# Two attention blocks over eight images: the last output projection by seven products, and other places in the order for the first job's steps

## The chip, the cores and the metric

The kernel runs on one core of a Trainium2 chip. The metric is the device time of one execution in microseconds (us); the median of several executions is compared. Everything is fp32. TensorE is called PE here, VectorE DVE, ScalarE ACT, GpSimd POOL and SyncE SP; SP does nothing but issue DMA transfers, and POOL does little besides issuing those that add to their destination.

## The reference, cut to what matters

The input x has 8 images of 512 channels and 1024 positions. Two blocks (layers 0 and 1) of the same form follow each other; only the names of the weights differ.

```python
# x: (8, 512, 1024); 8 groups; 8 heads of 64 channels
xn = (xg - mean) * rsqrt(var + 1e-5)            # over each group of 64 channels
xn = xn * gamma + beta
q, k, v = Wq @ xn + bq, Wk @ xn + bk, Wv @ xn + bv
attn = softmax(q^T k / 8)                        # per head, 1024 x 1024
o = attn @ v
x = x + Wp @ o + bp
```

## The kernel before, in words

**Jobs.** One job is one layer of one image, 16 in all. They run in pairs of images: (image b, layer 0), (b+1, layer 0), (b, layer 1), (b+1, layer 1) for b = 0, 2, 4, 6. Job n is counted from 0. A fast path assumes that softmax needs no subtraction of the maximum; a small check at the end (`judge`, L895 to L904) tells whether the sums stayed in range.

**Stages of a job.** (1) Attention of job n (`Attention`, L744 to L891): 64 steps of 1.71 us on the planner's clock. Each step has 4 score products (L764), one exponential of a 128x1024 tile on ACT (L769, tile `e`), one add of that tile to a running sum on DVE (L779, L781), and 4 value products (L795). Every 8 steps a group ends (`finish`): the sums are reduced (L811), the output goes into the tile that held q (L818), and for each second group the reciprocals go by DMA through DRAM (tiles `r`, `rd`) into a broadcast tile `rb` (two transfers at L857) and L872 multiplies by it. In the very last group all this is done on DVE alone, without DMA. (2) The V projection of job n+1 (`v_phase`, products at L462). (3) The output projection (O) of job n and then the K and Q projections of job n+1 (`deep_phases`, products at L593). Then attention of job n+1 begins.

**Products.** A projection is computed as a 2x2 block product with 7 half-size products in place of 8. `ORDER` (1, 5, 6, 2, 7, 3, 4) is the order in which they run so that few accumulators (banks z, y, u, v) are needed: z takes products 1, 6, 7 and 4, with copies to y after 1 and to u after 6; product 5 has a bank of its own; 2 goes into y, 3 into u. V does so at one level. O, K and Q do it at two: 7 outer products (`OUTER`, 1, 2, 6, 5, 7, 3, 4), each a *chain* of 7 inner ones with a tile `p_c`, where c = 0 to 20 counts the chains of O, K, Q. So for O the tile p_0 holds product 1, p_1 product 2, p_2 product 6, p_3 product 5, p_4 product 7, p_5 product 3 and p_6 product 4. The tiles `p_c` and `e` share one pool of 6 buffers. The second half of a chain's result is written from PSUM by DVE (L607, L609), the first by ACT. Weights and their sums are loaded or made once per layer, kept in DRAM (`keep` for one level, `deep` for two), and fetched into a ring of 7 tiles `w`.

**Adding O's products to x.** x is cut into quarters (half of the channels, half of the positions). `end(c)` says which products go into which quarter: 1 and 2 into (0,0); 6 (with 1 added), 5 and 3 into (0,1); 5 and 7 into (1,1); 7 (with 6 added) and 4 into (1,0). `more(...)` does one such addition: on DVE (L638, a thunk put at the end of the list `outer`), or, with `moved=True`, as an accumulating DMA of 512 KB issued by POOL (L636), which is written down at once. The lists `soon`, `outer` and `extra` give up one thunk at each of two places per chain (after inner products 7 and 3), `soon` before `outer` before `extra`. Every add is thereby written down some chains after its product ends. Two accesses to the same quarter wait for each other in the order in which they are written down.

**What sets the order.** The orders of PE, ACT and DVE instructions are the order in which the Python code issues them. Each engine runs its own list in that order. `later(delay, fn)` puts `fn` on the planner's clock, and `advance(us)` moves that clock on, so that small steps fall between products. `chores` is a table from attention steps to functions, filled by `put(i, fn)` (the next free step if i is taken). SP's and POOL's orders follow from a scheduler.

**Group norm of job 1.** It is done in job 0's attention, as job 1's image is loaded late: sums and squares on ACT (L239, L247), the channels' sums through DRAM to a tile of 8 groups, the group statistics on DVE (L270 to L274) and POOL (L275), out again through DRAM (`dg`, L277) and back as a broadcast (`mr`, L280), scale and offset on DVE (L288 to L290), and four applications on ACT (L295) that write `xn`. The sums `combine` over `xn` and the inner sums (`deep_steps`) follow. In the same attention DVE makes the weight sums of two more factors (L152 to L158, tile `raw`), and each set is stored as a 1.79 MB `keep` (L162).

**The end.** The last job's output projection is `plain_proj`: 64 products of 128x512 with the weights as they are (L733), a DVE addition of bias and x for each of 8 pieces (L737), and a store of each (L741).

Of the kernel before, what the change touches and what calls it, by code (L numbers as in the profile page):

```python
# [9 lines left out]
F32 = mybir.dt.float32  # L10
# [8 lines left out]
P = 128  # L19
B, C, H, W = 8, 512, 32, 32  # L20
# [6 lines left out]
NC = C // P  # L27
NT = S // P
HALF = S // 2
# [7 lines left out]
CH = C // 2  # L37
A11, S3, A12, A22, S1, S2, S4 = range(7)
NW = 7
K, V, Q, O = range(4)  # L40
FACTOR = {1: A11, 2: A12, 3: S4, 4: A22, 5: S1, 6: S2, 7: S3}
ORDER = (1, 5, 6, 2, 7, 3, 4)
OUTER = (1, 2, 6, 5, 7, 3, 4)
QT = HALF // 2
# [26 lines left out]
def fast_path(  # L71
# [10 lines left out]
    nc = tc.nc  # L82
# [8 lines left out]
    ps, turns = {}, [0]  # L91
# [14 lines left out]
    def later(delay, fn):  # L106
        todo.append((clock[0] + delay, fn))

    def advance(us):
        clock[0] += us  # L110
        due = sorted((t for t in todo if t[0] <= clock[0]), key=lambda t: t[0])
        for t in due:
            todo.remove(t)
            t[1]()
# [15 lines left out]
    def bank(half, tag, name):  # L130
        return ps[half][1].tile([P, HALF], F32, tag=tag, name=name)
# [80 lines left out]
    def load_x(b):  # L212
        for cc in range(NC):
            nc.sync.dma_start(xs[b][:, cc, :], x[b, cc * P : (cc + 1) * P, :])
# [316 lines left out]
    def deep_phases(n, extra, outs=None, early=()):  # L531
# [81 lines left out]
        def end(c):  # L613
            which, o = chains[c]
            m = job(which)
            used((m, which, o))

            def p(k):
                return tiles[which, k]

            def add(to_, a, b):
                outer.append(lambda: nc.vector.tensor_add(to_, a, b))  # L622

            if which == O:
                b, layer = jobs[m]
                xt = xs[b]

                def more(oh, sh, part, moved=False):


                    cols = slice(sh * HALF, (sh + 1) * HALF)
                    to_ = xt[:, 2 * oh : 2 * oh + 2, cols]

                    def go():
                        if moved:
                            nc.gpsimd.dma_start(to_, p(part), accum_op=ALU.add)  # L636
                        else:
                            nc.vector.tensor_add(to_, to_, p(part))  # L638
                        parts[oh, sh] -= 1
                        if layer == 1 and parts[oh, sh] == 0:  # L640
                            rows = slice(oh * CH, (oh + 1) * CH)
                            later(8.0 if moved else 2.0, lambda: nc.sync.dma_start(
                                out[b, rows, cols].rearrange("(c p) s -> p c s", p=P), to_
                            ))

                    if moved:
                        go()
                    else:
                        outer.append(go)

                if o == 1:
                    more(0, 0, 1, True)
                elif o == 2:
                    more(0, 0, 2, True)
                elif o == 6:
                    add(p(6), p(6), p(1))
                    more(0, 1, 6)
                elif o == 5:
                    more(0, 1, 5)
                    more(1, 1, 5, m in (0, 2))  # L660
                elif o == 7:
                    add(p(7), p(7), p(6))
                    more(1, 0, 7)
                    more(1, 1, 7)
                elif o == 3:
                    more(0, 1, 3, True)
                elif o == 4:
                    more(1, 0, 4, True)
                return
            d = dst[which]  # L670

            def quarter(oh, sh):
                return d[:, 2 * oh : 2 * oh + 2, sh * HALF : (sh + 1) * HALF]

            if o == 2:
                add(quarter(0, 0), p(1), p(2))
            elif o == 6:
                add(p(6), p(6), p(1))
            elif o == 5:
                add(quarter(0, 1), p(6), p(5))  # L680
            elif o == 7:
                add(p(7), p(7), p(6))
                add(quarter(1, 1), p(7), p(5))
            elif o == 3:
                add(quarter(0, 1), quarter(0, 1), p(3))
            elif o == 4:
                add(quarter(1, 0), p(7), p(4))
# [27 lines left out]
        at = sorted((7 * c + 2 * j, c, j) for c in range(len(chains)) for j in range(7))  # L715
        return [thunk(c, j) for _, c, j in at]

    def plain_weights(n):
        layer = jobs[n][1]
        w = acts.tile([P, NC, C], F32, tag="deep", name="w_last")  # L720
        nc.sync.dma_start(w, wp[layer].rearrange("(cc p) o -> p cc o", p=P))
        return w

    def plain_proj(n, w):

        b, layer = jobs[n]
        xt = xs[b]
        for sh in range(2):
            cols = slice(sh * HALF, (sh + 1) * HALF)
            for oc in range(NC):  # L730
                ps = bank(sh, "zyuv"[oc], f"pp_{n}_{sh}_{oc}")
                for cc in range(NC):
                    nc.tensor.matmul(  # L733
                        ps, w[:, cc, oc * P : (oc + 1) * P], qt[0][:, cc, cols],
                        start=(cc == 0), stop=(cc == NC - 1),
                    )
                nc.vector.scalar_tensor_tensor(  # L737
                    xt[:, oc, cols], ps, out_bias[:, layer, oc : oc + 1], xt[:, oc, cols],
                    ALU.add, ALU.add,
                )  # L740
                nc.sync.dma_start(out[b, oc * P : (oc + 1) * P, cols], xt[:, oc, cols])  # L741
                advance(3.5)

    class Attention:  # L744
        def __init__(self, n):
# [303 lines left out]
    t = sums(0)  # L1049
# [71 lines left out]
    for n in range(-1, len(jobs)):  # L1121
        last = n + 1 == len(jobs)
        outs = None
        if n >= 0:
            chores = {}

            def put(i, fn):
                while i in chores:
                    i += 1
                chores[i] = fn  # L1130

            if last:
                w = plain_weights(n)
            else:
                if n == 0:
                    first_factors(put, [(O, 0), (V, 1)])
                elif n == 1:
                    first_factors(put, [(K, 1), (Q, 1)])
                elif n == 2:
                    first_factors(put, [(O, 1)])  # L1140
                for i, (_, fn) in enumerate(extra):
                    put(2 + i, fn)
                at = (10, 19, 22, 24, 26, 28, 36, 39, 42, 45)
                if n == 0:
                    for i, fn in zip((3, 3, 4, 5, 6, 8, 10, 11, 12, 13, 15), reads):
                        put(i, fn)
                    at = (22, 30, 34, 35, 37, 38, 41, 44, 47, 50)
                for i, fn in zip(at, steps + sums(n + 1)):
                    put(i, fn)
                deep_first = deep_steps(n + 1)  # L1150
                for at, fn in zip((52, 54, 57, 59), deep_first[4:]):
                    put(at, fn)
                put(61, lambda: (extend_plan(n + 1), [fetch() for _ in range(RING)]))
            assert max(chores, default=0) < NT * len(att.groups)
            att.run(chores)
            banks(0, "one")
            banks(1, "one")
            if last:
                advance(100.0)
                advance(100.0)  # L1160
                judge()
                plain_proj(n, w)
                break
            outs = OutputSums(n)
            out_sums(n, outs)
            first = v_phase(n + 1, ORDER)
            for thunk in first[:-1]:
                thunk()
            rest = first[-1:]
            extra = deque()  # L1170
            if jobs[n][1] == 1 and jobs[n][0] + 2 < B:
                extra.append((11, lambda b=jobs[n][0] + 2: (x_tile(b), load_x(b))))
            if n == 1:
                load, bias_steps = make_out_bias(1)
                extra.append((8, load))
                extra.extend((11, fn) for fn in bias_steps)
            if n + 2 < len(jobs):
                reads, steps = norm_steps(n + 2)
                extra.extend((15, fn) for fn in reads)
        both = deep_phases(n + 1, extra, outs, deep_first[:4] if outs else ())  # L1180
        both[0]()
        rest[0]()
        if n < 0:
            later(22.0, lambda: load_x(1))
        for thunk in both[1:-2]:
            thunk()
        banks(0, "two")
        att = Attention(n + 1)
        att.scores(0)
        att.scores(1)  # L1190
        for thunk in both[-2:]:
            thunk()
        banks(1, "two")
# [249 lines left out]
```

## Time and profile before

| | |
|---|---|
| median of 10 runs | 3216.35 us (3214.45 to 3218.15) |
| profiled execution: its time, its span | 3216.58 us, 3214.8 us |
| PE busy | 3194.4 us (99%), clock 1.000 |
| DVE, ACT, POOL busy | 2767.3 (86%), 1902.4 (59%), 99.5 us (3%) |
| DMA | 313.04 MB, mean 97 GB/s |
| first score product of job 0 | 82.86 us |
| first products of the last projection | 3181.31 us |

In the lines of a timeline the columns are the start in us, the busy time in us, the engine, the line of the kernel, the operation with its output and inputs, shapes and count, and in brackets the idle time of that engine before it and what ended it. SPq lines are transfers being issued by SP. A chain's lines are the start, the length and the engine or transfer that the end of the execution depended on in that stretch.

### The profile page before, as it was taken

To read this page: it belongs to the slowest core of one execution; us is meant where nothing else is said; L and a number is where in the kernel's file an instruction comes from. 1 tells how busy PE (TensorE), PEld (TensorE's weight loads), DVE (VectorE), ACT (ScalarE), POOL (GpSimd) and SP (SyncE) were. 2 spreads that over 40 slices of the span, in tenths; PEclk is the share of its full clock that TensorE was granted. 3 is DMA by queue.
4 is the path that set the end of the run, shared out by engine and by line. 5 is a ranking of instruction groups with operands and counts; after the bars stand their busy time and mean duration, and the time that the engine had idled before them with its cause. 6 is when DMAs were issued, how large, how long until landed. Compare 5 with 4: busy or idle time off the path is not lost.

```text
span 3214.8 us, 57636 instructions
## 1 busy us (share of the span) xinstructions
PE 3194.4 (99%) x22870; PEld 1850.1 (58%) x22870; DVE 2767.3 (86%) x3958; ACT 1902.4 (59%) x3038; POOL 99.5 (3%) x93
## 2 busy tenths in 40 slices
PE   9999999999999999999999999999999999999999
PEld 7366384563836638366483754837557374573843
DVE  8897998979889798897988889888897888988876
ACT  4746646466565665656656565565656656566563
POOL 0000000000000000000000000000000000000000
PEclk9999999999999999999999999999999999999999
DMA  8234172350613305034160421505216051150501
GB/s 316 97 104 130 68 210 69 93 170 22 209 28 88 90 27 158 22 104 127 33 210 16 118 67 38 147 16 144 93 45 192 16 142 43 55 130 22 173 22 41
DMA packets 149462, 313.04 MB, mean 97 GB/s; under 512 B 33864, under 2 KB 46784, under 8 KB 148160
## 3 DMA queue, kind: packets, MB, share of 16 engines
q1 hardware_dynamic: 132320, 276.77, 26.8%
q0 software_dynamic: 16864, 32.51, 6.2%
q8 instruction: 181, 2.97, 0.4%
q14 instruction: 97, 0.79, 0.1%
HBM read 224.35 MB, written 51.18 MB: 86 GB/s over the span
## 4 chain that ended last, share of the span: by engine, by line
PE 95%; DVE 3%; DMA 1%; issue 0%; SPq 0%; ACT 0%; DVEq 0%
PE sc L764 28%; PE po L795 27%; PE vd L593 10%; PE zd L593 10%; PE z L462 6%; PE ud L593 4%; PE yd L593 4%; PE v L462 2%; PE y L462 2%; PE u L462 2%; PE pp L733 1%; DMA x<-p 0%; DMA w<-wqkv_dram 0%; DVE w L154 0%; DVE p L609 0%; DMA raw_v<-wqkv_dram 0%
## 5 line engine op out<-in xcount | busy, mean ns | idle before, releaser
L769 ACT ACTIVATE e<-sc 128x1024 f32<-128x1024 f32 x1024 | 1045.9, 1023 | 582.4 <-PE sc L764 487.4
L764 PE MATMUL sc<-q,k 64*64 64x512 f32 x8192 | 1061.7, 590 | 0.0
L795 PE MATMUL po<-e,v 64*64 64x512 f32 x8192 | 1057.2, 589 | 0.0
L781 DVE TENSOR_TENSOR acc<-acc,e 128x1024 f32<-128x1024 f32 x768 | 936.3, 1219 | 57.7 <-ACT e L769 8.8
L795 PEld LDWEIGHTS po<-e,v 64*64 64x64 f32 x8192 | 313.0, 133 | 566.0 <-issue 557.5
L764 PEld LDWEIGHTS sc<-q,k 64*64 64x64 f32 x8192 | 309.7, 133 | 559.1 <-issue 545.4
L593 PE MATMUL vd<-deep,w 128*128 128x256 f32 x900 | 252.6, 380 | 1.4 <-DVE p L609 1.3
L593 PE MATMUL zd<-deep,w 128*128 128x256 f32 x892 | 248.4, 380 | 5.0 <-DVE p L607 2.2
L779 DVE TENSOR_TENSOR acc<-e,e 128x1024 f32<-128x1024 f32 x128 | 156.4, 1222 | 111.3 <-ACT e L769 111.3
L593 PEld LDWEIGHTS zd<-deep,w 128*128 128x128 f32 x892 | 168.9, 190 | 30.4 <-DVE p L607 3.5
L593 PEld LDWEIGHTS vd<-deep,w 128*128 128x128 f32 x900 | 170.6, 190 | 26.4 <-DVE p L609 2.5
L811 DVE TRANSPOSE_TENSOR_REDUCE r<-acc 128x32 f32<-128x1024 f32 x128 | 158.5, 1238 | 0.5
L636 POOL DMA_DIRECT2D x<-p x62 | 74.6, 1211 | 1972.2 <-ACT p L603 1408.1
L593 PE MATMUL vd<-os,w 128*128 128x256 f32 x420 | 118.1, 380 | 1.6 <-DVE p L609 1.5
L622 DVE TENSOR_TENSOR p<-p,p 128x1024 f32<-128x1024 f32 x94 | 114.2, 1215 | 0.0
L462 PE MATMUL z<-w,t 128*128 128x256 f32 x480 | 110.9, 379 | 0.0
L462 PE MATMUL z<-w,xn 128*128 128x256 f32 x480 | 110.1, 382 | 0.0
L413 ACT COPY ud<-vd 128x256 f32<-128x256 f32 x173 | 61.8, 357 | 77.2 <-PE vd L593 69.8
L611 ACT COPY s<-zd 128x256 f32<-128x256 f32 x173 | 64.5, 373 | 71.8 <-PE zd L593 71.7
L475 ACT COPY v<-z 128x512 f32<-128x512 f32 x32 | 18.7, 585 | 148.5 <-PE z L462 148.5
L462 PEld LDWEIGHTS z<-w,xn 128*128 128x128 f32 x480 | 90.0, 190 | 23.8 <-issue 12.2
L413 ACT COPY ud<-zd 128x256 f32<-128x256 f32 x156 | 55.7, 357 | 76.6 <-PE zd L593 75.1
(213 smaller groups left out, 4058.0 us busy)
## 6 DMA issues: line engine op xcount, KB each, us to landing
w<-deep SPq DMA_DIRECT2D x287, 448.0 KB, 3.9
w<-keep SPq DMA_DIRECT2D x129, 256.0 KB, 2.7
x<-p POOLq DMA_DIRECT2D x62, 512.0 KB, 6.6
rb<-rd SPq DMA_DIRECT2D x96, 256.0 KB, 4.1
deep<-w SPq DMA_DIRECT2D x42, 448.0 KB, 3.7
x<-x_dram SPq DMA_DIRECT2D x28, 512.0 KB, 4.5
out_dram<-x SPq DMA_DIRECT2D x28, 512.0 KB, 6.2
keep<-raw SPq DMA_DIRECT2D x5, 1792.0 KB, 7.7
```

The costliest lines, as they stand in the source:

```text
L413: nc.scalar.copy(u, z)
L462: nc.tensor.matmul(ps[:, ti * CH : (ti + 1) * CH], r[:, cc, t0 : t0 + P], w[:, cc, :], start=(start and ti == 0 and cc == 0), stop=(cc == ...
L593: nc.tensor.matmul(ps, lhs[:, FACTOR[i], :], moving[i], start=start, stop=True, skip_group_check=True,)
L611: return chain(product, lambda ps: nc.scalar.copy(s5, ps), put, z, y, u, w)
L622: outer.append(lambda: nc.vector.tensor_add(to_, a, b))
L636: nc.gpsimd.dma_start(to_, p(part), accum_op=ALU.add)
L764: nc.tensor.matmul(sc[h * HD : (h + 1) * HD, j, :], k[r, hp, k0 : k0 + HD], q[r, hp, sh * HALF : (sh + 1) * HALF], start=True, stop=True,)
L769: nc.scalar.activation(e, sc, AF.Exp, scale=SCALE)
L779: nc.vector.tensor_add(acc[g], self.es[i - 1], e)
L781: nc.vector.tensor_add(acc[g], acc[g], e)
L795: nc.tensor.matmul(po[g][j * HD : (j + 1) * HD, h, :], v[r, kc, d0 : d0 + HD], e[r, j, :], start=(kc == 0), stop=(kc == NT - 1),)
L811: nc.vector.tensor_reduce(self.r[:, 0, m, :], self.acc.pop(g).rearrange("p j (b e) -> p (j b) e", e=RP), AX.X, ALU.add, apply_transpose=True,)
```

## The change

It has five parts.

1. The last job's output projection is done by seven products of half size, by halves of the positions (`last_weights`, `last_right`, `last_sums`, `last_proj`). The weights are the kept factors of layer 1, of one level. For each half, 7 products of 8 matmuls of 128x256; ORDER and the banks as elsewhere. The four sums of the first half's positions are chores at steps 44, 47, 50 and 53 of the last attention; those of the second half and `judge` are put on the planner's clock during the projection.
2. The second image's load is put at 32 rather than 22 us on the planner's clock of the first K and Q phase.
3. In job 0's attention the group statistics, the factors, the four applications and the four sums stand at steps 20, 30, 31, 32, 34, 35, 36, 38, 40, 43 (before 22, 30, 34, 35, 37, 38, 41, 44, 47, 50), and the inner sums at 45, 47, 51, 53 (before 52, 54, 57, 59).
4. For m = 0 and 2 (`fresh`), products 1 and 2 are added to quarter (0,0) by DVE through `outer` rather than by a DMA; product 7 is added to (1,1) by a DMA that is itself put into `outer`. For the other jobs nothing changes.
5. The steps that make layer 1's output bias move from the phase after job 1's attention to the one after job 0's.

```diff
--- before.py
+++ after.py
@@ -648,20 +648,24 @@
                     else:
                         outer.append(go)
 
+                fresh = m in (0, 2)
                 if o == 1:
-                    more(0, 0, 1, True)
+                    more(0, 0, 1, not fresh)
                 elif o == 2:
-                    more(0, 0, 2, True)
+                    more(0, 0, 2, not fresh)
                 elif o == 6:
                     add(p(6), p(6), p(1))
                     more(0, 1, 6)
                 elif o == 5:
                     more(0, 1, 5)
-                    more(1, 1, 5, m in (0, 2))
+                    more(1, 1, 5, fresh)
                 elif o == 7:
                     add(p(7), p(7), p(6))
                     more(1, 0, 7)
-                    more(1, 1, 7)
+                    if fresh:
+                        outer.append(lambda: more(1, 1, 7, True))
+                    else:
+                        more(1, 1, 7)
                 elif o == 3:
                     more(0, 1, 3, True)
                 elif o == 4:
@@ -715,31 +719,84 @@
         at = sorted((7 * c + 2 * j, c, j) for c in range(len(chains)) for j in range(7))
         return [thunk(c, j) for _, c, j in at]
 
-    def plain_weights(n):
-        layer = jobs[n][1]
-        w = acts.tile([P, NC, C], F32, tag="deep", name="w_last")
-        nc.sync.dma_start(w, wp[layer].rearrange("(cc p) o -> p cc o", p=P))
+    def last_weights(n):
+        w = acts.tile([P, NW, 2, CH], F32, tag="deep", name="w_last")
+        nc.sync.dma_start(w, factors[O, jobs[n][1]])
         return w
 
-    def plain_proj(n, w):
+    def last_right(sh, o):
+
+        at = slice(sh * QT, (sh + 1) * QT)
+        if o in (4, 5, 6):
+            return tx[0][:, {5: 0, 6: 1, 4: 2}[o], :, at]
+        rows = 0 if o in (1, 7) else 2
+        cols = 2 * sh + (0 if o in (1, 2) else 1)
+        return qt[0][:, rows : rows + 2, cols * QT : (cols + 1) * QT]
+
+    def last_sums(sh):
+
+
+        def start():
+            if sh == 0:
+                tx[0] = acts.tile([P, 3, 2, HALF], F32, tag="t", name="t_last")
+            nc.vector.tensor_sub(last_right(sh, 5), last_right(sh, 7), last_right(sh, 1))
+
+        def second():
+            nc.vector.tensor_sub(last_right(sh, 6), last_right(sh, 3), last_right(sh, 5))
+
+        def third():
+            nc.vector.tensor_sub(last_right(sh, 7), last_right(sh, 3), last_right(sh, 7))
+
+        def fourth():
+            nc.vector.tensor_sub(last_right(sh, 4), last_right(sh, 2), last_right(sh, 6))
+
+        return start, second, third, fourth
+
+    def last_proj(n, w, sh):
 
         b, layer = jobs[n]
         xt = xs[b]
-        for sh in range(2):
-            cols = slice(sh * HALF, (sh + 1) * HALF)
-            for oc in range(NC):
-                ps = bank(sh, "zyuv"[oc], f"pp_{n}_{sh}_{oc}")
-                for cc in range(NC):
+        z, y, u, w5 = (bank(sh, t, f"{t}_last_{sh}") for t in "zyuv")
+
+        def product(o, ps, start):
+            r = last_right(sh, o)
+            for oc in range(2):
+                for cc in range(2):
                     nc.tensor.matmul(
-                        ps, w[:, cc, oc * P : (oc + 1) * P], qt[0][:, cc, cols],
-                        start=(cc == 0), stop=(cc == NC - 1),
+                        ps[:, oc * QT : (oc + 1) * QT],
+                        w[:, FACTOR[o], cc, oc * P : (oc + 1) * P], r[:, cc, :],
+                        start=(start and oc == 0 and cc == 0), stop=(cc == 1),
+                        skip_group_check=True,
                     )
+
+        def quarter(oh, ph):
+            p0 = sh * HALF + ph * QT
+            return xt[:, 2 * oh : 2 * oh + 2, p0 : p0 + QT]
+
+        def chunks(ps):
+            return ps.rearrange("p (a e) -> p a e", a=2)
+
+        def put5(ps):
+            for oh in range(2):
+                nc.vector.tensor_add(quarter(oh, 1), quarter(oh, 1), chunks(ps))
+
+        def put(oh, ph, ps):
+            to_ = quarter(oh, ph)
+            for a in range(2):
+                oc = 2 * oh + a
                 nc.vector.scalar_tensor_tensor(
-                    xt[:, oc, cols], ps, out_bias[:, layer, oc : oc + 1], xt[:, oc, cols],
+                    to_[:, a], chunks(ps)[:, a], out_bias[:, layer, oc : oc + 1], to_[:, a],
                     ALU.add, ALU.add,
                 )
-                nc.sync.dma_start(out[b, oc * P : (oc + 1) * P, cols], xt[:, oc, cols])
-                advance(3.5)
+                nc.sync.dma_start(
+                    out[b, oc * P : (oc + 1) * P, sh * HALF + ph * QT : sh * HALF + (ph + 1) * QT],
+                    to_[:, a],
+                )
+
+        step = chain(product, put5, put, z, y, u, w5)
+        for o in ORDER:
+            step(o)
+            advance(1.72)
 
     class Attention:
         def __init__(self, n):
@@ -1130,7 +1187,9 @@
                 chores[i] = fn
 
             if last:
-                w = plain_weights(n)
+                w = last_weights(n)
+                for i, fn in enumerate(last_sums(0)):
+                    put(44 + 3 * i, fn)
             else:
                 if n == 0:
                     first_factors(put, [(O, 0), (V, 1)])
@@ -1144,11 +1203,11 @@
                 if n == 0:
                     for i, fn in zip((3, 3, 4, 5, 6, 8, 10, 11, 12, 13, 15), reads):
                         put(i, fn)
-                    at = (22, 30, 34, 35, 37, 38, 41, 44, 47, 50)
+                    at = (20, 30, 31, 32, 34, 35, 36, 38, 40, 43)
                 for i, fn in zip(at, steps + sums(n + 1)):
                     put(i, fn)
                 deep_first = deep_steps(n + 1)
-                for at, fn in zip((52, 54, 57, 59), deep_first[4:]):
+                for at, fn in zip((45, 47, 51, 53) if n == 0 else (52, 54, 57, 59), deep_first[4:]):
                     put(at, fn)
                 put(61, lambda: (extend_plan(n + 1), [fetch() for _ in range(RING)]))
             assert max(chores, default=0) < NT * len(att.groups)
@@ -1156,10 +1215,11 @@
             banks(0, "one")
             banks(1, "one")
             if last:
-                advance(100.0)
-                advance(100.0)
-                judge()
-                plain_proj(n, w)
+                for i, fn in enumerate(last_sums(1)):
+                    later(4.1 + 1.5 * i, fn)
+                later(9.9, judge)
+                for sh in range(2):
+                    last_proj(n, w, sh)
                 break
             outs = OutputSums(n)
             out_sums(n, outs)
@@ -1170,7 +1230,7 @@
             extra = deque()
             if jobs[n][1] == 1 and jobs[n][0] + 2 < B:
                 extra.append((11, lambda b=jobs[n][0] + 2: (x_tile(b), load_x(b))))
-            if n == 1:
+            if n == 0:
                 load, bias_steps = make_out_bias(1)
                 extra.append((8, load))
                 extra.extend((11, fn) for fn in bias_steps)
@@ -1181,7 +1241,7 @@
         both[0]()
         rest[0]()
         if n < 0:
-            later(22.0, lambda: load_x(1))
+            later(32.0, lambda: load_x(1))
         for thunk in both[1:-2]:
             thunk()
         banks(0, "two")
```

## The prediction

> **What bounds the kernel now.** I read the page's busy shares and chain first. Below, m is the job whose projection is added to x, and L numbers are those of the kernel before unless marked.
>
> ```profile
> PE 3194.4 (99%) x22870; PEld 1850.1 (58%) x22870; DVE 2767.3 (86%) x3958; ACT 1902.4 (59%) x3038; POOL 99.5 (3%) x93
> PE 95%; DVE 3%; DMA 1%; issue 0%; SPq 0%; ACT 0%; DVEq 0%
> ```
>
> PE is the limit; 214.8 − 194.4 = 20.4 us of idle is all that ordering can return, and what lies ahead of the first product is part of it. Where the idle lies is told by stage windows between the first score products of successive jobs (columns: stretch, length, then PE, PEld, DVE, ACT, POOL busy, clock, DMA share, GB/s):
>
> ```profile
> 82.93:288.18 205.25, 200.24 (x1434) 115.17 (x1436) 179.16 (x273) 126.87 (x208) 8.27 (x6) 1.00 0.38 115
> 288.18:491.20 203.02, 200.31 (x1435) 115.18 (x1437) 188.69 (x310) 119.14 (x192) 6.22 (x5) 1.00 0.42 129
> 491.20:691.60 200.40, 199.12 (x1434) 115.55 (x1438) 178.29 (x269) 119.22 (x192) 7.43 (x6) 1.00 0.40 124
> 691.60:889.81 198.21, 198.21 (x1434) 115.94 (x1437) 170.62 (x237) 119.25 (x192) 6.22 (x5) 1.00 0.34 99
> ```
>
> From the fourth on PE is never idle: nothing can be won there. The first three are 7.0, 4.8 and 2.2 us over 198.21; with the ends these are what the change touches. PE's timeline names the stalls in brackets, and the last projection:
>
> ```profile
> 200.74 1.99 PE L462 MATMUL v<-w,t 128*128 128x256 f32 x8 [1.09 <-DVE q L818]
> 245.10 0.70 PE L593 MATMUL zd<-deep,w 128*128 128x256 f32 x2 [1.05 <-ACT yd L409]
> 250.36 0.70 PE L593 MATMUL zd<-deep,w 128*128 128x256 f32 x2 [1.54 <-DVE p L607]
> 3181.31 27.73 PE L733 MATMUL pp<-q,w_last 128*128 128x512 f32 x64
> ```
>
> DVE's timeline tells why the 250.36 stall exists, and shows the other places the change touches:
>
> ```profile
> 73.85 0.29 DVE L152 TENSOR_TENSOR w<-w 128x128 f32<-128x128 f32 x1 [1.58 <-DMA w<-wqkv_dram]
> 122.85 0.59 DVE L842 TENSOR_REDUCE lt<-r 32x64 f32<-32x256 f32 x1 [1.94 <-DMA r<-r]
> 132.99 1.19 DVE L872 TENSOR_TENSOR q<-q,rb 128x1024 f32<-128x1024 f32 x1
> 248.75 1.23 DVE L638 TENSOR_TENSOR x<-x,p 128x1024 f32<-128x1024 f32 x1 [2.42 <-DMA x<-p]
> 249.89 0.42 DVE L607 TENSOR_TENSOR p<-zd,s 128x256 f32<-128x256 f32 x1
> ```
>
> An add to x stood 2.42 us for an accumulating DMA into the same quarter, the bank read (L607) stood behind it, and PE behind that. In the chain it is `DMA x<-p` at 236.95, 11.78 us long. SP's own timeline:
>
> ```profile
> 127.48 1.29 SPq L857 DMA_DIRECT2D rb<-rd  x2
> 128.81 0.59 SPq L162 DMA_DIRECT2D keep<-raw  x1
> 131.76 0.28 SPq L277 DMA_DIRECT2D dg<-ga  x1
> 136.41 1.11 SPq L280 DMA_DIRECT2D mr<-dg  x2
> ```
>
> dg is a few bytes, issued behind the 1.79 MB keep, and mr, which waits for it, goes out 4.6 us later. The same dg in job 1's attention, with no keep ahead, takes 1.2 us (311.82 to 312.99).
>
> **The Trainium skill.** "TensorE: Matmul & The Clock Gate" (Architectural detail) says ACT and DVE are strict FIFO: the trace agrees (L607 behind L638, above). "DMA: Bandwidth & Descriptors" (Queues, rings and completion order) says descriptors of one ring are consumed in order, and each DMA engine takes turns between rows at packet level. The 4.6 against 1.2 us agrees, and so do the accumulates of POOL: 7.8 to 11.8 us at m=0 where the 16 DMA engines are busy over 90% (224 to 256 us), 5.6 to 6.6 typically in later jobs. Its "Rules for kernel authors" says an access to bytes that an accumulating DMA touches must wait for its semaphore; so the adds on DVE must wait, and the trace shows one that does. Its SWDGE fit, 2.0 us + bytes/436e3, would give 3.2 us for 512 KB; the trace never shows under 5.4, and I use the trace.
>
> **The change, part by part.**
>
> *Last projection.* Removed: 64 records, 27.73 us. Added: 112 records of 128x256. An x16 row of such records advances PE 3.45 us (L462 rows at 202.57 and 206.02), so 112 take 24.2. DVE's chain before them (r, q, rb, q) ends 7.2 us after the start, at 3188.4; then two 0.60 adds for product 5, sums and puts (0.60, 2×0.40, 0.60, 2×0.40) release bank z at about +11.2, while PE wants it for product 4 at +10.35: 0.9 stall. The last two puts are 2×0.44 against one of 0.75: +0.13. Net −27.73 + 24.2 + 0.9 + 0.13 = −2.5; I take **−2.3** (−3 to −1.5). The eight sums on DVE cost nothing on the path: four lie in job 15's attention, where DVE waits 1.5 to 2.2 us per group for exponentials, four are in the chain just counted. Weights of 1.8 rather than 1.0 MB load a whole attention ahead. What follows the last put (issue 0.33, landing 2.4, end 2.4 us) stays.
>
> *x(1) loaded 10 us later.* A weight load issued at 64.97 landed at 73.8 behind four x loads of SP (62.12 to 64.35); DVE waited 1.58 and PE then 1.27 at 75.33 (its restart costs 0.1 more). The new SP order has the weight ahead of x: **−1.4**. x then lands near 78; its first reader (ACT L239) starts at 91.3, so that cover is 13 us.
>
> *Job 0's attention steps.* DVE has no idle from 122.85 to 236.95, so an order of the same DVE instructions alone gains only what fills the 1.94 at 122.85 (the group statistics, 0.8). But two queues change. (1) SP now issues dg and mr, then keep, then the two rb; before, rb went ahead of keep. keep moved data until 135.3 in before; issued at about 127.4 it ends near 134, and rb behind it lands near 136.9 (135 to 138.5). L872 (after: L929) would be ready at 132.2: waits 4.7, less the 0.8 gained, **+3.9** for all of DVE behind it. (2) On ACT the first normalise (L295) moves from behind exponential 35 to behind exponential 32. It waits for `off` (L290), 143.2 in before, now 147.1; exponential 32 ends at 139.5. Exponential 33, and with it DVE's next add and PE's next products, stands behind. Together about +6.2 (4.4 to 7.9), less any slack: none on DVE, which sets PE's stalls at 200.74, 228.11 and 232.04, so it is passed on: **+6.2**. Lower bound −0.8, were neither wait there.
>
> *x += p at m = 0 and 2.* Products 1 and 2 leave POOL (two accumulates of 512 KB less) for two DVE adds of 1.13 each; one DVE add of product 7 leaves for POOL. DVE +1.1 per job, covered only as far as it has idle. More important is the order. The accumulates of products 3 and 4 (tiles p_5, p_6) are recorded when their product ends, but the longer list of DVE adds is still being popped one at a time. So in the instruction order after, DVE has x += p_3 waiting for the p_5 accumulate into the same quarter, and two adds later x += p_4 waiting for that of p_6. p_5 in turn is issued only when the previous add to its quarter is done, just ahead; p_6 when its own second half is written, which stands behind x += p_3. Both landings therefore lie in series on DVE, L5 and L6. Behind the two adds stand the bank reads L607 of p_7 and L609 of p_8, and PE's zd and vd products behind those. DVE does 2.1 us of other work within the landings and would without the waits be 1.2 ahead of PE: loss L5 + L6 − 3.3. m=0: p_5 goes out at about 243.4, in the saturated stretch: L5 = 8.0 (7.8 to 9.2 seen there); by p_6 the stalled SP stream drains, L6 = 6.2 (as later jobs). 10.9, less the stalls removed (1.05, 1.54, 0.2 restarts) = **+8.1**. m=2: p_5 at 649.65, where the nearest accumulate (648.99) took 10.0; with one fewer beside it 9.3; 9.3 + 6.2 − 3.3 = **+12.2** (7.8 to 16); nothing was waiting there before.
>
> *Output bias of layer 1 one job earlier.* Four 0.68 us multiply-sums (L970, 464 to 477) leave job 1's K/Q phase, whose PE waits of 0.63 and 0.38 (at 469.94 and 483.60, restarts counted) go: **−1.1**, part of it doubtful. They land in 262 to 285, where DVE idles 0.5 to 1.1 per chain. One statistics step moves into job 1's attention: **+0.3**.
>
> Sum: −2.3 − 1.4 + 6.2 + 8.1 + 12.2 − 1.1 + 0.3 = **+22.0**. The profiled run of before was 3216.58 (span 3214.8 and 1.8 around it), 0.23 above the median 3216.35; I add the difference to the median: **3238**. All low ends together give about +10, all high ones +31.
>
> **Rivals.**
> (a) *The adds do not wait; the change does what it says.* The accumulates would have to land within about 0.5 us of their issue, or DVE have that much other work. Then −2.3 − 1.4 − 2.8 (stalls at m=0) − 2.4 (start of job 0) − 1.1 = −10: **3206**, faster. Against: the smallest landing seen is 5.4; turning point: L5 + L6 under about 3.3 and no rb wait.
> (b) *rb is not held by keep* (its packets take turns): job 0 gives +1.5 from the moved normalise alone: **3233**. For: rb reads DRAM in another pattern. Against: dg's 4.6.
> (c) *Only one add waits in earnest, or both landings are 5.4.* With 5.4 twice, m=0 and 2 lose 3.4 and 4.7 less (3230); with L6 hidden, 6.2 less each (3226): **3228**.
> (d) *Landings of 11 and 8 in both,* since the SP stream does not drain: 15.7 in place of 10.9 and 12.2: **3246**.
>
> **How the numbers follow.** Main case 0.50, (b) 0.15, (c) 0.17, (d) 0.10, (a) 0.04, mixtures near zero 0.04. 0.2% is 6.4 us, about what a measurement of this kernel can tell. Faster 0.04 (a), same 0.04, slower 0.92. Range 3223 to 3248: the main case's own bounds, with (b), (c), (d).
>
> **What would show it.** In after's trace: DVE adds L638 at m=0 and 2 with `<-DMA x<-p` of about 7 and 5 us each, PE stalls of 7 and more behind them; a wait of 4 to 5 us for `rb` at L929 near 132, and ACT L295 ahead of exponential 33 waiting; the stage windows at about 219.5, 202, 212.5 and then 198.21 unchanged; the last products 25 us. If the second add waits under 1 us, the series argument is wrong; if stage one is under 207, both queues were misread.

## The result, and the profile after

The kernel after takes 3235.58 us (median of 8 runs, 3234.38 to 3237.43); the kernel before, run beside it, 3215.95 (28 runs, 3214.36 to 3220.52). The ratio is 1.0061, 95% interval 1.0053 to 1.0070: slower by 19.6 us. The profiled execution took 3237.88 us with a span of 3236.0. It is 2.3 us above its median, and most of that lies behind the last instruction on DVE: 3236.0 − 3229.33 = 6.67 us here, against 3214.8 − 3209.84 = 4.96 before and 4.4 to 4.9 in the traces of the eleven other kernels below, which have the same new end. One execution of all those reported, of the kernel with keep later, took 5229 us for a reason that is not known; the intervals leave it out.

The page's first row and its row of clocks (tenths of full speed in 40 slices) look almost as before, as an average over 3236 us must:

```profile
PE 3195.9 (99%) x22918; PEld 1861.8 (58%) x22918; DVE 2777.2 (86%) x3980; ACT 1904.9 (59%) x3042; POOL 95.6 (3%) x91
PEclk9999999999999999999999999999999999999999
```

The stage windows between first score products tell where the time is (stretch, length, busy time of PE, PEld, DVE, ACT, POOL, clock, DMA share, GB/s):

```profile
81.60:301.60 220.00, 203.57 (x1432) 115.92 (x1431) 182.47 (x283) 127.14 (x208) 5.53 (x5) 0.97 0.37 111
301.60:502.75 201.15, 199.28 (x1431) 115.48 (x1431) 187.09 (x302) 119.15 (x192) 6.22 (x5) 1.00 0.41 124
502.75:713.31 210.56, 201.76 (x1432) 117.15 (x1431) 178.84 (x269) 119.25 (x192) 6.26 (x5) 0.98 0.38 116
713.31:911.52 198.21, 198.21 (x1432) 115.94 (x1431) 170.62 (x237) 119.26 (x192) 6.22 (x5) 1.00 0.34 99
```

Against before: start −1.26 (82.86 to 81.60; the program ran 0.27 late already at 46 us, so the later load is worth 1.53), first stage +14.75, second −1.87, third +10.16, the fourth equal to the hundredth, and from the first product of the last projection to the end of its last put 26.24 for 28.53, −2.29. The sum is +19.5. PE's timeline names the stalls (stretches in which PE stands still), in brackets:

```profile
147.34 1.98 PE L821 MATMUL sc<-q,k 64*64 64x512 f32 x8 [5.92 <-ACT e L826]
...
260.65 1.22 PE L593 MATMUL zd<-deep,w 128*128 128x256 f32 x2 [8.06 <-DVE p L607]
...
266.87 0.70 PE L593 MATMUL vd<-deep,w 128*128 128x256 f32 x2 [1.19 <-DVE p L609]
...
672.36 1.22 PE L593 MATMUL zd<-deep,w 128*128 128x256 f32 x2 [7.00 <-DVE p L607]
...
3214.33 1.99 PE L765 MATMUL z_last<-t_last,w_last 128*128 128x256 f32 x8 [0.61 <-DVE x L787]
```

And DVE's timeline tells what PE stood for. At m = 0:

```profile
248.35 0.47 DVE L609 SCALAR_TENSOR_TENSOR p<-zd,out_bias,s 128x256 f32<-128x256 f32 x1
257.51 1.22 DVE L638 TENSOR_TENSOR x<-x,p 128x1024 f32<-128x1024 f32 x1 [8.68 <-DMA x<-p]
258.65 0.48 DVE L609 SCALAR_TENSOR_TENSOR p<-ud,out_bias,s 128x256 f32<-128x256 f32 x1
259.05 1.21 DVE L622 TENSOR_TENSOR p<-p,p 128x1024 f32<-128x1024 f32 x1
260.18 0.42 DVE L607 TENSOR_TENSOR p<-zd,s 128x256 f32<-128x256 f32 x1
264.86 1.23 DVE L638 TENSOR_TENSOR x<-x,p 128x1024 f32<-128x1024 f32 x1 [4.27 <-DMA x<-p]
```

Two adds, two waits, one behind the other, and in between the bank reads that PE wants. At m = 2 the same pair waits 7.62 and 4.27 us. In job 0's attention there are two more, on DVE for rb and on ACT for the offset, and behind the second DVE waits for the exponential (147.32):

```profile
134.81 1.23 DVE L929 TENSOR_TENSOR q<-q,rb 128x1024 f32<-128x1024 f32 x1 [3.72 <-DMA rb<-rd]
...
144.94 0.16 DVE L290 TENSOR_TENSOR off<-vec_sb,off 128x4 f32<-128x4 f32 x1
...
147.32 1.23 DVE L836 TENSOR_TENSOR acc<-e,e 128x1024 f32<-128x1024 f32 x1 [2.22 <-ACT e L826]
```

```profile
137.27 1.02 ACT L826 ACTIVATE e<-sc 128x1024 f32<-128x1024 f32 x1 [0.71 <-DVE acc L838]
145.14 1.24 ACT L295 ACTIVATE xn<-x,off,mul 128x1024 f32<-128x1024 f32 x1 [6.84 <-DVE off L290]
146.28 1.00 ACT L826 ACTIVATE e<-sc 128x1024 f32<-128x1024 f32 x1
```

The second fence is ACT's timeline: exponential 32, then the normalise, then exponential 33, which PE's 5.92 us stand for. SP's timeline has the order as forecast, mr and keep ahead of rb:

```profile
123.59 1.75 SPq L280 DMA_DIRECT2D mr<-dg  x2
125.44 0.54 SPq L162 DMA_DIRECT2D keep<-raw  x1
126.08 2.05 SPq L914 DMA_DIRECT2D rb<-rd  x2
```

### The profile page after: what moved, and what is told of

It reads as the page before. It is cut to its first block, busy times and chain, and to the rows that moved or that the text cites. A ratio compares the mean times of both kernels' runs of the same rounds, so it can differ in the third digit from the quotient of the medians.

```text
span 3236.0 us, 57775 instructions
## 1 busy us (share of the span) xinstructions
PE 3195.9 (99%) x22918; PEld 1861.8 (58%) x22918; DVE 2777.2 (86%) x3980; ACT 1904.9 (59%) x3042; POOL 95.6 (3%) x91
## 4 chain that ended last, share of the span: by engine, by line
PE 78%; DVE 1%; issue 0%; DMA 0%; ACT 0%; DVEq 0%; POOLq 0%
PE sc L821 22%; PE po L852 22%; PE vd L593 9%; PE zd L593 9%; PE z L462 5%; PE ud L593 4%; PE yd L593 4%; PE y L462 1%; PE u L462 1%; PE v L462 1%; PE z_last L765 0%; DVE acc L838 0%; DMA x<-p 0%; DVE q L929 0%; DVE x L787 0%
## 5 line engine op out<-in xcount | busy, mean ns | idle before, releaser
L638 DVE TENSOR_TENSOR x<-x,p 128x1024 f32<-128x1024 f32 x75 | 91.1, 1215 | 24.8 <-DMA x<-p 24.8
L462 PEld LDWEIGHTS z<-w,xn 128*128 128x128 f32 x480 | 90.0, 190 | 23.8 <-issue 12.2
```

Of the source, the lines that this page charges most:

```text
L462: nc.tensor.matmul(ps[:, ti * CH : (ti + 1) * CH], r[:, cc, t0 : t0 + P], w[:, cc, :], start=(start and ti == 0 and cc == 0), stop=(cc == ...
```

## The experiments

In all of them the times of before are of runs on the same chips (medians 3216.12 to 3216.26). "Stage" is a window as above.

**Part 4 undone.**

```diff
-                fresh = m in (0, 2)
+                fresh = False
-                    more(1, 1, 5, fresh)
+                    more(1, 1, 5, m in (0, 2))
```

> After, with part 4 (x += p at m = 0 and 2) undone. Theory (two adds on DVE wait in series for accumulating DMAs, PE stands behind): job 0's stage loses 8.4 us of its 220.0, the third stage returns to about 200.4 (from 210.6); about 3217, PE's stalls of 8.06 and 7.00 gone and the old ones of 1.05 and 1.5 back. Rival (the loss at m = 0 is carried over from the attention steps, as DVE comes late): m = 0 stays long, only the third stage recovers: about 3225.

3217.39 us, ratio 1.0002 (0.9994 to 1.0011). First stage 211.51, third 200.11: 8.49 and 10.45 us less. The stalls of 8.06 and 7.00 are gone, the old ones at m = 0 are back (1.94 and 1.05, where before has 1.05 and 1.54). The loss at m = 0 is its own and not carried over.

**Part 3 undone.**

```diff
-                    at = (20, 30, 31, 32, 34, 35, 36, 38, 40, 43)
+                    at = (22, 30, 34, 35, 37, 38, 41, 44, 47, 50)
-                for at, fn in zip((45, 47, 51, 53) if n == 0 else (52, 54, 57, 59), deep_first[4:]):
+                for at, fn in zip((52, 54, 57, 59), deep_first[4:]):
```

> After, with part 3 (the steps of job 0's attention) undone. Theory (rb behind keep in SP's queue, then a normalise ahead of an exponential): job 0's attention recovers about 6.35 us, PE's stall of 5.92 at 147 gone, the adds at m = 0 and 2 still wait as long: about 3229. Rival (DVE is the limit in job 0 and what one place saves the next one takes): under 2 us gained, about 3234.

3230.49 us, ratio 1.0044 (1.0027 to 1.0061). The stall at 147 is gone, the first stage is 213.62 (6.38 less), and the pair of waits at m = 0 is 8.40 and 4.28 as in after. The rival's gain of under 2 us is out.

**Parts 3 and 4 undone** (both edits).

> After, with parts 3 and 4 undone: the last projection by seven products, the later load of x(1) and the earlier bias remain. Theory: these give -2.3, -1.3 and about -1.5, so 3210 to 3212, faster than before by 4 to 6 us. Rival (the later load or the bias cost something that the two large losses hid): 3214 to 3217.

3211.74 us, ratio 0.9987 (0.9980 to 0.9993): 4.4 us faster than before. Stages 206.15, 201.15, 200.13. Parts 1, 2 and 5 together are a gain, and no loss of theirs was hidden behind the two large ones. Part 5 has a run of its own below; parts 1 and 2 were not run apart, and their shares are read from the traces.

**The same work, the DMAs written down in turn.** The transfers of products 3 and 4 also go through `outer`.

```diff
                 elif o == 3:
-                    more(0, 1, 3, True)
+                    if fresh:
+                        outer.append(lambda: more(0, 1, 3, True))
+                    else:
+                        more(0, 1, 3, True)
                 elif o == 4:
-                    more(1, 0, 4, True)
+                    if fresh:
+                        outer.append(lambda: more(1, 0, 4, True))
+                    else:
+                        more(1, 0, 4, True)
```

> After, with the accumulating DMAs of products 3 and 4 also put through the list outer at m = 0 and 2, so that they are written down behind the adds on DVE. Same amount of work on every engine. Theory (the order makes the waits, not the work): no wait of DVE for x<-p over 1 us, the third stage about 200.4, job 0's stage about 209 to 211 (6.35 for the attention steps left): 3214 to 3219. Rival (the extra DVE adds or the shared DMA engines make the loss): above 3228.

3217.56 us, ratio 1.0005 (0.9996 to 1.0014); stages 211.72 and 201.06, where after has 220.00 and 210.56. Every engine has the same instructions. The order alone is worth 18 us. Its DVE timeline, with after's two waiting adds now among the rest:

```profile
249.02 1.22 DVE L638 TENSOR_TENSOR x<-x,p 128x1024 f32<-128x1024 f32 x1
250.15 0.48 DVE L609 SCALAR_TENSOR_TENSOR p<-ud,out_bias,s 128x256 f32<-128x256 f32 x1
250.55 1.22 DVE L622 TENSOR_TENSOR p<-p,p 128x1024 f32<-128x1024 f32 x1
251.68 0.41 DVE L607 TENSOR_TENSOR p<-zd,s 128x256 f32<-128x256 f32 x1
252.01 1.21 DVE L638 TENSOR_TENSOR x<-x,p 128x1024 f32<-128x1024 f32 x1
...
264.70 0.42 DVE L607 TENSOR_TENSOR p<-zd,s 128x256 f32<-128x256 f32 x1 [2.02 <-DMA x<-p]
```

No add waits. What is left are two late buffers: twice a `p` tile is written again 1.8 to 2.4 us late, by DVE (at 264.70 and 269.33) and by ACT (at 264.69 and 269.32), because the DMA that reads it has not landed. This costs PE 0.87 and 1.45 us. So even in this order part 4 gains nothing over part 4 undone (3217.56 against 3217.39): it trades one late transfer for another.

**Only the second add in turn**, with part 3 undone (compare with 3230.49): the edit above for product 4 alone.

> Part 3 undone (3230.5 with only that); the accumulating DMA of product 4 alone goes through outer at m = 0 and 2, that of product 3 still ahead of the add on DVE. Theory (two landings in series): the first wait of 7.6 to 8.7 stays, the second of 4.3 us goes. As PE's stall after the second one was only 1.2 to 1.4, because most of it fell while PE worked again, each job gains 1.0 to 1.5: about 3228. Rival (the waits are one: the second only takes what the first leaves): the first grows and nothing is gained, 3230.

3228.71 us, ratio 1.0038 (1.0023 to 1.0052). That is 1.8 us below 3230.49, but the ranges overlap (3227.6 to 3230.36 in 5 runs, 3229.03 to 3231.72 in 4). The second wait is gone, but at m = 0 the first was 9.93 us here (its DMA landed after 9.7 us, in the other run after 8.2):

```profile
252.90 1.23 DVE L638 TENSOR_TENSOR x<-x,p 128x1024 f32<-128x1024 f32 x1 [9.93 <-DMA x<-p]
255.90 1.22 DVE L638 TENSOR_TENSOR x<-x,p 128x1024 f32<-128x1024 f32 x1
```

PE's stall is 9.31 where the two were 7.78 and 1.38. At m = 2 the first landing hardly differs (8.6 us, in the other run 8.5), and there the first wait stays at 8.81 for 8.64: it does not take over what the second leaves, as the rival had it. PE's stall is 8.19 for 8.02 and 1.25, yet the stage is only 0.64 us shorter (210.97 for 211.61), since PE is at half speed just there (see the part on why the prediction was right). The first wait is what costs; the second adds little to the time.

**Keep later than rb.** With part 4 undone (3217.39) the fourth sum of the first stored factor and its store come five steps later.

```diff
-                put(at, lambda i=i, part=part: factor(box[0][:, i], part))
-            put(at + 1, lambda i=i, which=which, layer=layer: store_factors(
+                put(at + (5 if at == 21 and which_layers[0] == (O, 0) else 0), lambda i=i, part=part: factor(box[0][:, i], part))
+            put(at + (6 if at == 21 and which == O and layer == 0 else 1), lambda i=i, which=which, layer=layer: store_factors(
```

> Part 4 undone (as the run with only that), and job 0's last sum for the first stored factor, with its keep store, five attention steps later, so that SP issues both rb ahead of keep. Theory (keep ahead of rb in one queue makes the wait of 3.7 us at L929): that wait is under 0.5 us; the normalise L295 still stands ahead of exponential 33, but its offset is ready near 141.2, so ACT waits about 3 us instead of 6.8 and PE about 2 instead of 6: job 0's stage about 207, 3212 to 3214. Rival (rb is slow by itself): the wait stays over 3 us, 3217.

3213.91 us, ratio 0.9994 (0.9985 to 1.0003); first stage 208.35, 3.2 less. The wait for rb is 0.66, ACT waits 4.16 us in place of 6.84 and PE 3.16.

**Normalises later.** Part 4 undone, keep as in after.

```diff
-                    at = (20, 30, 31, 32, 34, 35, 36, 38, 40, 43)
+                    at = (20, 30, 34, 35, 36, 37, 38, 39, 40, 43)
```

> Part 4 undone, and the four normalises at steps 34 to 37 rather than 31 to 36 with gaps (sums and inner sums as in the change); keep stays ahead of rb. Theory (two waits in series): the wait for rb stays 3.7 us, the ACT wait of 6.8 goes to under 3.5 (the offset is ready at 145, exponential 35 now ahead of it), PE's stall of 6 becomes 1 to 3: job 0's stage about 207 to 209, 3213 to 3216. Rival (DVE's 3.7 us alone make the whole loss, as DVE has no idle): no gain, 3217.

3215.39 us, ratio 0.9998 (0.9990 to 1.0007); first stage 208.64. The wait for rb stays (4.21), ACT waits 2.19, PE 1.19 there and 2.46 at the end of the attention.

**Both edits.**

> Part 4 undone, with both edits: keep after rb, and the normalises later. Theory: neither wait left; job 0's stage equals that of old steps (206.15) or 0.8 less, as the group statistics fill an idle stretch of DVE: 3210.5 to 3212. Rival (the earlier sums themselves cost): above 3214.

3211.63 us, ratio 0.9987 (0.9980 to 0.9994). First stage 206.40, no stall of PE in the attention's middle. Old steps give 206.15, in a stage that had no half clock of PE, as this one has (last section). The medians, 3211.63 and 3211.74 with 20 runs each, can't be told apart: the earlier sums cost nothing and bring nothing that these runs show.

**Keep from POOL.** Part 4 undone; this was to test the prediction's reason for rb's delay, that SP's queue holds it.

```diff
-        nc.sync.dma_start(keep, w)
+        (nc.gpsimd if (which, layer) == (O, 0) else nc.sync).dma_start(keep, w)
```

> Part 4 undone, the steps of part 3 kept, but the 1.79 MB keep store of job 0's attention is issued by POOL, so that it isn't in SP's queue. The same bytes move at the same time. Theory (order within SP's queue): the wait of DVE for rb at L929 falls from 3.7 us to under 1.5, PE's stall from 6 to about 3. Rival (the DMA engines' time is what lacks): the wait stays over 3 us.

3218.29 us (one run). The wait did not fall. POOL's and DVE's timelines:

```profile
125.44 0.76 POOL L162 DMA_DIRECT2D keep<-raw  x1 [4.38 <-DVE raw L158]
```

```profile
135.16 1.23 DVE L929 TENSOR_TENSOR q<-q,rb 128x1024 f32<-128x1024 f32 x1 [4.11 <-DMA rb<-rd]
```

rb, now with no large transfer ahead of it on SP, took 8.2 us from issue to landing, against 8.0 in after; DVE's wait was 3.80 with part 4 alone undone. The theory as predicted fails here: it isn't the place in SP's queue. rb is late beside the 1.79 MB of keep whichever of the two queues carries them. That the later keep takes the wait to 0.66, and the other queue doesn't, leaves the time of the DMA engines themselves, or of the memory behind them; that is found by elimination, and no run here tells the two apart.

**The bias back.** Parts 3, 4 and 5 undone.

```diff
-            if n == 0:
+            if n == 1:
                 load, bias_steps = make_out_bias(1)
```

> Parts 3, 4 and 5 undone: only the last projection and the later load of x(1). Theory (the bias moved is worth about 1 us): the second stage back at 203.0 from 201.15, the first at 205.25 from 206.15, the start and the end as after: about 3212.7, that is 1 us slower than with the bias moved. Rival (the bias steps' loads are what made the first stage 0.9 longer, and the second gains nothing): 3211 or less.

3212.72 us, ratio 0.9989 (0.9980 to 0.9998). Stages 205.09, 203.04, 200.12 against 206.15, 201.15, 200.13 with the bias moved: 1.9 won in the second, 1.1 given back in the first, 0.8 net; the medians differ by 1.0.

**Product 7 by DMA at m = 0 alone**, on the run with both edits.

```diff
-                    if fresh:
+                    if m == 0:
                         outer.append(lambda: more(1, 1, 7, True))
```

> The run with keep later and the normalises later (3211.6), and at m = 0 product 7 added to (1,1) by a DMA in the order of outer, products 1 and 2 as before the change. One add on DVE fewer (1.13 us), one DMA more. Theory (at m = 0 the adds wait for DMAs, so a DVE add fewer helps only where no buffer comes late): between 3210 (the stall for the add gone) and 3214 (a late buffer in its place). Rival (more accumulates slow one another): over 3215.

3211.37 us, ratio 0.9985 (0.9978 to 0.9992); first stage 205.72, for 206.40. It can't be told from 3211.63. It, the run with both edits, and parts 3 and 4 undone are three forms of the fastest kernel here, 4.4 to 4.9 us below before.

## Why the prediction was right

The sign and the size were right (+22.0 forecast, +19.6 measured), and so was the mechanism of the large losses: adds on DVE that wait for transfers written down ahead of them, and PE behind DVE. The order in which DVE, ACT and SP would run their work came out as forecast. The terms compare as follows.

| term | predicted | measured | from |
|---|---|---|---|
| last projection | −2.3 | −2.29 | 28.53 to 26.24 in the profiles |
| x(1) later | −1.4 | −1.5 | from the product at 46.08 (after: 46.35) to the first score product, 36.78 to 35.25; the stall at 75.33 is gone |
| job 0's steps | +6.2 | +6.4 or +5.4 | 220.0 − 213.62 with part 4, 211.51 − 206.15 without |
| m = 0 | +8.1 | +8.5 | 220.00 − 211.51 |
| m = 2 | +12.2 | +10.45 | 210.56 − 200.11 |
| bias | −0.8 | −0.8 | both stages, run with the bias back |

Some of this closeness is luck, as errors inside the terms cancel.

*Three of the four landings were taken too long, and too much work was taken to lie within them.* L5 and L6 are the landings of the transfers of `p_5` and `p_6`. L5 was 8.5 us at m = 0 for the 8.0 taken, but 7.5 at m = 2 for 9.3, and L6 was 5.1 us in both for 6.2, shorter than any landing in before's trace (5.3 there, where the prediction has 5.4). The 10.0 us of the one at 648.99 in before was not a guide; there the next accumulate went out 3.1 us behind it, in after 9.6 us behind, but no run tests whether that is the reason. On the other side the prediction took 2.1 us of DVE's other work to lie within the landings. It was 0.7 us: the landings add up to 13.6 and 12.6 us, DVE's waits to 12.95 and 11.89. With the measured landings and the 2.1 us left in, the formula gives 7.5 for m = 0 and 9.3 for m = 2, both about 1 us short. DVE's waits less the 1.2 us by which it was taken to be ahead give 11.75 and 10.7, and at m = 0 the old stalls go off that (1.94 and 1.05 in the run without part 4, restarts 0.2): 8.6 and 10.7, for 8.5 and 10.45 measured.

*PE's half clock was not foreseen, but is not a term on top.* Windows over the records behind the stalls at 147.34 and 260.65, with the clock in the third column from the right:

```profile
147.30:149.10 1.80, 1.76 (x9) 0.55 (x13) 1.78 (x2) 1.38 (x2) 0.00 (x0) 0.50 0.00 0
149.10:150.80 1.70, 1.70 (x12) 0.49 (x8) 1.70 (x4) 1.35 (x2) 0.00 (x0) 0.50 0.00 0
...
262.00:264.20 2.20, 2.20 (x6) 1.69 (x6) 0.00 (x0) 1.11 (x3) 0.10 (x1) 0.50 1.11 185
264.20:266.00 1.80, 1.48 (x7) 0.95 (x5) 1.14 (x1) 0.37 (x1) 0.00 (x0) 1.00 1.07 146
```

PE ran at half speed for 3.5 to 5 us. From 260.65 four pairs of products took 3.57 us (to 264.22) where a restart (the first pair behind a stall) and three more pairs take 0.53 + 3 × 0.43 = 1.83 at full speed: 1.7 us more. At 672.36 six pairs took 5.07 for 2.68, 2.4 us more. The Trainium skill has this ("TensorE: Matmul & The Clock Gate", Part 1: The HAM clock gate: half rate after an idle window of about 3.4 us, full rate after as much busy time; here shorter stalls were enough at times, see the last section). The prediction counted stalls as if PE came back at full speed. The page's row of clocks, in tenths, does not show it. PE's own account of m = 2 needs it: 7.00 + 0.55 of stall, 2.4 of slow clock and two restarts of 0.1 are 10.2 of the 10.45. Yet at 266.87 and 678.58 PE stood once more for DVE, and between the two stalls DVE waited for the second landing alone (4.27 us), not for PE. By these traces a PE at full speed would only have stood longer there, and the loss would be the same; no run tests this apart. Where the second wait is missing, as in the run with only the second add in turn, the slow products take its place: at m = 2 six pairs took 5.08 us there, and most of what the second stall had cost was not won.

*The reason for rb's wait was wrong, its size nearly right.* Predicted 4.7, measured 3.72. "rb goes behind keep in SP's queue" is refuted by the run with keep on POOL; what the runs leave is that both move at once. The small transfer dg in before, which led to that reading, fits either account. The other half, a normalise ahead of an exponential on an engine that runs its list in order, is shown twice: later normalises take PE's stall from 6 to 1.2 us, and a keep that is later takes it to 3.16, since the offset is then ready sooner. The two waits are in one chain, so each edit alone saves about 3 us and both together 5.1. DVE's waits again account for the term: 3.72, the 2.22 at 147.32 (2.3 forecast) and one of 1.01 for a later rb at 194.89 that was not forecast, less 0.7 of the old wait at 122.85 that is filled (0.8 forecast), are 6.3 of the 6.4.

*The bias is right by two errors.* The second stage won 1.9 where 1.1 was forecast, and the first gave back 1.1 where 0.3 was.

Of the rivals, the clean case (a) fell with the first two DVE lines; (b) was right in its reason for doubt, as rb isn't held by a queue, and wrong in its number; (c) is half true: both adds wait, but by the run with only the second add in turn nearly the whole loss of m = 0 and 2 hangs on the first; (d) fell with the landings, 8.5 and 5.1 us at the longest for 11 and 8.

## What to carry to other kernels

An add that is moved from a DMA to an engine changes the order in which accesses to one buffer are written down; if a transfer to the same buffer is already ahead, an in-order engine inherits the whole landing time, and everything behind it too. Write such transfers through the same list as the adds. Ahead of a step that is moved earlier, ask what else moves bytes at that time: here a large store delayed a small broadcast from both queues that were tried. Behind a stall of PE of 3 us or more expect some 2 us of work lost to a half clock (1.7 to 2.4 here); count it only where PE does not soon stand again for the engine that it had waited for.

## What the runs showed of the hardware that was not expected

- The half clock of PE came with every stall from 3.16 us up (3.16, 5.92 and all longer ones). Of the shorter ones it followed some: 1.79 us (at 15.38, run with the bias back, which makes that trace's start late), 1.92 (product 7 by DMA at m = 0) and 2.39 (run with both edits), in the last case only 1.4 us after PE had started again. Others it did not follow: 2.46 (normalises later), 1.94 (part 4 undone) and 1.79 (parts 3 and 4 undone). So in this range the length of a stall alone does not tell. In the lines below, of the run with both edits and of the one with normalises later, two pairs take 1.71 us (247.09 to 248.80) behind the shorter stall, where full speed is 0.43 a pair, and the sixteen products behind the longer one run at full speed:

```profile
244.83 0.70 PE L593 MATMUL zd<-deep,w 128*128 128x256 f32 x2 [2.39 <-ACT yd L409]
...
247.09 1.91 PE L593 MATMUL zd<-deep,w 128*128 128x256 f32 x4
```

```profile
203.03 1.99 PE L462 MATMUL v<-w,t 128*128 128x256 f32 x8 [2.46 <-DVE q L875]
204.86 3.62 PE L462 MATMUL z<-w,t 128*128 128x256 f32 x16
```

- After the stall of 3.16 us eight score products took 1.76 us in place of 0.86.
- The broadcast rb, 4.1 us from issue to landing as the median of before's page, took 8.0 to 8.2 us beside a 1.79 MB store, from the same queue or from another.
- The same accumulate of 512 KB, with the same neighbours by the order of instructions, landed at m = 0 after 8.2 us in one execution (part 3 undone) and 9.7 in another (only the second add in turn); at m = 2 it took from 7.5 (after) to 8.6.
